# Routed rows placed in units of 128: 36 groups of two units in place of 39 groups of 256 rows

## The chip, the cores and the metric

The kernel runs on one core of a Trainium2 chip. A time is device microseconds (us) from start to end of one execution. Times are given as the median of several runs. The profile describes one further execution, with a time of its own. On the chip, TensorE (PE) does the matmuls, VectorE (DVE), ScalarE (ACT) and GpSimd (POOL) the elementwise work, and SyncE (SP) issues most of the DMA transfers. PEld is TensorE's loading of a matmul's stationary operand.

## The reference: what is computed

Two transformer layers on 8 x 512 tokens of width 256. Each layer adds attention and a mixture of experts to its input. In both layers every token goes to two of eight experts. Cut to what matters:

```python
def _L0_ffn_ref(x, Wg, Wu, Wd, W1, W2):            # F = 512
    topv, topi = top_k(softmax(xt @ Wg), 2)
    topv = topv / sum(topv)
    y = gelu(xt @ Wu[e]) @ Wd[e]                   # of the two experts chosen
    return gelu(xt @ W1) @ W2 + sum of y * weight

def _L1_ffn_ref(x, router_w, router_b, w1, b1, w2, b2):   # F = 1024
    top_w, sel = top_k(xf @ router_w + router_b, 2)
    gates = softmax(top_w)
    out_i = gelu(xf @ w1[i] + b1[i]) @ w2[i] + b2[i]
    return sum of out_i * gate_i over the two chosen

xn = layernorm(x);  x = x + L0_attn(xn) + L0_ffn(xn)
xn = layernorm(x);  x = x + L1_attn(xn) + L1_ffn(xn)
```

The 4096 tokens make 8192 routed rows in each layer. How many rows an expert gets is known only on the chip, so the number of groups that the program runs is the largest that could be needed.

## The kernel before, in words

**Routing.** `Routing.choose` finds each token's two experts on DVE. `Routing.places` (lines 291 to 367) counts the rows of each expert with two matmuls and a scan, rounds each expert's count up to groups of GT = 256 rows, and gives every routed row its place in a buffer in HBM (`xd`) in which each expert's rows begin at a multiple of 256. `NG_MAX` (line 36) is (8192 + 8 * 255) // 256 = 39 groups. `self.eid` holds each group's expert. `Routing.send` scatters the normalized rows to their places with 64 indirect DMAs of POOL per layer.

**One group** (`Experts`, lines 449 to 655). `load` reads the group's expert number into a register, loads that expert's weights as one tile of the tag `ew` (1024 KB in layer 0, 2180 KB with the biases in layer 1), and loads the group's 256 rows (`xg`; in layer 1 also `xe`, the rows' routing columns). `turn` transposes the rows (TensorE in layer 0, DVE in layer 1) and works out where the results go. `up` does the first matmul, one weight block of 128 x 128 against 256 columns of rows at a time, and the gelu on ACT (line 582 in layer 0, two blocks at once; line 578 in layer 1, one block, because of the bias). `down` does the second matmul for each half of 128 rows, scales by the gate, in layer 1 adds the bias `b2` out of the weight tile (line 616), and POOL scatters the result to HBM (line 625). A float32 matmul is two instructions ("passes") in the profile, so a group of layer 1 is 32 passes of `up` and 32 of `down`, and one of layer 0 16 and 16.

**Layer 0.** The groups are worked on between the steps of attention. A loop over n (lines 1033 to 1102) has one stage for each of 32 units of attention: four heads of one block of 512 tokens. In stage n the scores of unit n+1 are computed for their maxima (`maxima`, with DVE's reduction, line 836), and unit n's probabilities (`probs`, with ACT's exp, line 861), and between these stand other steps out of the deque `between`: norms, projections, the `down` of the groups of stage n-1, the `turn` of those of stage n. The `up` of stage n's groups comes at its end, and then the loads of the groups two further on. A stage begins with `shift(n)`, whose DVE subtraction is line 848. Groups of a shared expert fill the stages before 8 and after 27. `groups_of` (line 984) spreads the routed groups over stages 8 to 27: two for each stage, and one for stage 27. The routing of layer 0 is one step of stage 2.

**Layer 1.** Half of attention runs first (`attention1`, part "a", with the routing of layer 1 as one of its steps), then all groups in one stretch (`Experts.all`, lines 640 to 655), then the other half of attention. The program of that stretch is, for group i: the load of i+2, the turn of i+1, `up(i)`, `down(i-1)`. The weights' pool has three buffers (line 1387). A load that has no free buffer waits until the last reader of an earlier group's weights, line 616, is done. The order on each engine's queue is made when the program is built, from dependencies, priorities and expected times, so it can differ from the order in which the program writes its steps.

Of the kernel before, what the change touches and what calls it, by code (L numbers as in the profile page):

```python
# [17 lines left out]
P = 128  # L18
# [16 lines left out]
GT = 256  # L35
NG_MAX = (2 * B * S + E1 * (GT - 1)) // GT
TT = B * NT
# [10 lines left out]
C_THR = C_ONES + P  # L48
C_GRP = C_THR + B * S // GT
C_KEEP = C_GRP + NG_MAX  # L50
C_ROW = C_KEEP + TT
C_ALL = C_ROW + NG_MAX * GT // P

# [15 lines left out]
def tile_two_layers(  # L69
# [51 lines left out]
    ones = cs[:, C_ONES : C_ONES + P]  # L121
    thr = cs[:, C_THR : C_THR + B * S // GT]
    grp = cs[:, C_GRP : C_GRP + NG_MAX]
    keep = cs[:, C_KEEP : C_KEEP + TT]
    rowno = cs[:, C_ROW : C_ROW + NG_MAX * GT // P]

# [77 lines left out]
    class Routing:  # L204

        def __init__(self, layer):
            n = self.layer = layer
            self.asked, self.fetched = {}, set()  # L210
            self.sent, self.posted = [], []
            self.lg = rpool.tile([P, TT, 8], F32, tag="lg", name=f"lg{n}")
            self.hot = [
                rpool.tile([P, TT, 8], F32, tag=f"hot{k}", name=f"hot{n}_{k}") for k in range(2)
            ]

            self.of = rpool.tile([P, TT, 3, 2], F32, tag="of", name=f"of{n}")
            self.g = [rpool.tile([P, TT], F32, tag=f"g{k}", name=f"g{n}_{k}") for k in range(2)]
            self.pos = [rpool.tile([P, TT], I32, name=f"pos{n}_{k}") for k in range(2)]
            self.eid = rpool.tile([P, NG_MAX], I32, name=f"eid{n}")  # L220
            self.ef = rpool.tile([P, NG_MAX], F32, name=f"ef{n}")

            self.spare = rpool.tile([P, NG_MAX * GT // P], F32, tag="spare", name=f"spare{n}")
            self.xn_d = dpool.tile([B, P, NT, D], F32, name=f"xn_d{n}")
            self.xd = dpool.tile([NG_MAX * GT, XW], F32, name=f"xd{n}")
            self.zd = dpool.tile([1 + 2 * PLANE + NG_MAX * GT, D], F32, name=f"zd{n}")
# [64 lines left out]
        def places(self, ps_pool):  # L291


            def by_expert(ap):
# [14 lines left out]
            upto = self.small("upto", 8, TT)  # L309
            reset = self.small("reset", 8, TT)  # L310
            nc.vector.tensor_copy(reset, keep.unsqueeze(1).to_broadcast([P, 8, TT]))
# [7 lines left out]
            )  # L319
            m = B * S // GT  # L320
            over = self.small("over", 8, m)
            nc.vector.tensor_tensor(
                over,
                upto[:, :, TT - 1].unsqueeze(2).to_broadcast([P, 8, m]),
                thr.unsqueeze(1).to_broadcast([P, 8, m]),
                ALU.is_gt,
            )
            groups = self.small("groups", 8)
            nc.vector.tensor_reduce(groups, over, AX.X, ALU.add)
            end = self.small("end", 8)  # L330
            nc.vector.tensor_tensor_scan(end, ones[:, :8], groups, 0.0, ALU.mult, ALU.add)

            nc.vector.tensor_sub(groups, end, groups)
            nc.vector.scalar_tensor_tensor(
                upto,
                groups.unsqueeze(2).to_broadcast([P, 8, TT]),
                float(GT),
                upto,
                ALU.mult,
                ALU.add,  # L340
            )
            nc.vector.tensor_sub(upto, upto, tot)
            nc.vector.tensor_tensor(
# [3 lines left out]
                ALU.add,  # L347
            )
            for k in range(2):
                part = self.small("rest", TT, 8)  # L350
                nc.vector.tensor_tensor(
                    part, self.hot[k], upto.rearrange("p e t -> p t e"), ALU.mult
                )
                row = self.small("row", TT)
                nc.vector.tensor_reduce(row, part, AX.X, ALU.add)
                nc.vector.tensor_copy(self.pos[k], row)
            done = self.small("done", NG_MAX, 8)
            nc.vector.tensor_tensor(
                done,
                end.unsqueeze(1).to_broadcast([P, NG_MAX, 8]),  # L360
                grp.unsqueeze(2).to_broadcast([P, NG_MAX, 8]),
                ALU.is_le,
            )
            of = self.small("of", NG_MAX)
            nc.vector.tensor_reduce(of, done, AX.X, ALU.add)
            nc.vector.tensor_scalar_min(self.ef, of, 7.0)
# [82 lines left out]
    class Experts:  # L449


        def __init__(self, routing, e_d, wpool, pool, ps_x, ps_up, ps_dn, nf, bias, tag=None):
# [6 lines left out]
            self.post = lambda step: step()  # L459

        def load(self, i):
            r = self.r
            e = nc.sync.value_load(r.eid[0:1, i : i + 1], min_val=0, max_val=7)
            n_all = self.n_up + self.n_dn + (self.nf + D if self.bias else 0)
            w = self.wpool.tile([P, n_all], F32, tag="ew", name=f"ew{r.layer}_{i}")
            nc.sync.dma_start(w, self.e_d[bass.ds(e, 1)].rearrange("o p n -> p (o n)"))
            self.weights[i] = w
            if self.blocks:
# [57 lines left out]
        def address(self, i, of):  # L526
# [4 lines left out]
            mine = self.pool.tile([P, n_t, 2], F32, tag="mine", name=f"mine{n}_{i}")  # L531
            nc.vector.tensor_scalar(
                mine, of[:, :, 0], self.r.ef[:, i : i + 1], None, ALU.is_equal
            )
# [19 lines left out]
        def up(self, i, f2):  # L554
            n, w = self.r.layer, self.weights[i]
            wu = w[:, : self.n_up].rearrange("p (k f) -> p k f", k=KD)
            xt = self.xts[i]
            if f2 == 0:
                self.hts[i] = self.pool.tile(
                    [P, self.nf, GT], F32, tag="hgT", name=f"hgT{n}_{i}"  # L560
                )
            ht = self.hts[i]
            ps = self.ps_up.tile([P, 2, GT], F32, tag=self.tag[1], name=f"gup{n}_{i}_{f2}")
            for j in range(2):
                f = 2 * f2 + j
                for k in range(KD):
                    nc.tensor.matmul(  # L567
                        ps[:, j, :],
                        wu[:, k, f * P : (f + 1) * P],
                        xt[:, k],  # L570
                        start=(k == 0),
                        stop=(k == KD - 1),
                    )
            if self.bias:
                at = self.n_up + self.n_dn
                for j in range(2):
                    f = 2 * f2 + j
                    nc.scalar.activation(  # L578
                        ht[:, f, :], ps[:, j, :], AF.Gelu, bias=w[:, at + f : at + f + 1]
                    )  # L580
            else:
# [4 lines left out]
        def down(self, i, t, held={}):  # L586
            n, nf = self.r.layer, self.nf
            w = self.weights[i]
            wd = w[:, self.n_up : self.n_up + self.n_dn]
            wd = wd.rearrange("p (f d) -> p f d", f=nf)  # L590
            ht = self.hts[i]
# [13 lines left out]
            if t == GT // P - 1:  # L605
# [5 lines left out]
                for s in range(GT // P):  # L611
                    g = way[:, s, 1:2]
                    if self.bias:
                        nc.scalar.activation(y[:, s, :], ps[:, s, :], AF.Copy, scale=g)  # L614
                        b2 = w[:, self.n_up + self.n_dn + nf :]
                        nc.vector.scalar_tensor_tensor(  # L616
# [23 lines left out]
        def all(self):  # L640
            self.load(0)
            self.load(1)
            self.turn(0)
            for i in range(NG_MAX):
                if i + 2 < NG_MAX:
                    self.load(i + 2)
                if i + 1 < NG_MAX:
                    self.turn(i + 1)
                for f2 in range(self.nf // 2):
                    self.up(i, f2)  # L650
                if i:
                    for t in range(GT // P):
                        self.down(i - 1, t)
            for t in range(GT // P):
                self.down(NG_MAX - 1, t)

# [68 lines left out]
    with tc.tile_pool(name="l0w", bufs=1) as awp, tc.tile_pool(  # L725
# [254 lines left out]
        shared = deque(("shared", i) for i in range(B * S // GT))  # L980
        experts = deque(("routed", i) for i in range(NG_MAX))
        FIRST, LAST = 8, 27
# [43 lines left out]
        def loading():  # L1026
            move(len(moves))
            routed.load(0)
            routed.load(1)

        norms = deque(s for b in range(1, B) for s in norm_steps(b))
        downs = []
        for n in range(-1, N + 1):
# [57 lines left out]
            for group in groups:  # L1091
# [3 lines left out]
                kind, i = group  # L1095
                if kind == "routed" and i + 2 < NG_MAX:
                    routed.load(i + 2)
            if FIRST < n <= FIRST + CLEAR:
# [287 lines left out]
    attention1(list(range(B // 2)), "a", before, lambda b: None)  # L1386
    with tc.tile_pool(name="m1w", bufs=3) as wp, tc.tile_pool(
        name="m1", bufs=2
# [7 lines left out]
def _shape_constants():  # L1396
# [12 lines left out]
    c[:, C_ONES : C_ONES + P] = 1.0  # L1409
    c[:, C_THR : C_THR + B * S // GT] = GT * np.arange(B * S // GT)  # L1410
    c[:, C_GRP : C_GRP + NG_MAX] = np.arange(NG_MAX)
    c[:, C_KEEP : C_KEEP + TT] = np.arange(TT) > 0
    c[:, C_ROW :] = P * np.arange(NG_MAX * GT // P)[None, :] + p[:, None]

# [78 lines left out]
```

## Time and profile before

| | us |
|---|---|
| median of 3 runs | 2071.28 |
| the 3 runs | 2068.76, 2071.28, 2080.68 |
| the profiled execution, its own time | 2069.25 |
| its span, first to last instruction | 2067.6 |

| stretch of the profiled execution | us | PE busy | granted TensorE clock |
|---|---|---|---|
| 0 to 320: set-up, first stages of layer 0's attention, shared groups | 320 | 265.20 | 0.95 |
| 320 to 930: stages with the routed groups of layer 0 | 610 | 589.38 | 0.99 |
| 930 to 1060: last stages, adding the routed results, norms | 130 | 92.53 | 0.81 |
| 1060 to 1319: attention of layer 1, part a | 259 | 215.24 | 0.88 |
| 1319 to 1330: wait for the first rows and weights | 11 | 0.00 | 0.56 |
| 1330 to 1873: the groups of layer 1 | 543 | 542.80 | 1.00 |
| 1873 to 2067.6: attention of layer 1, part b | 194.6 | 169.08 | 0.97 |

A line of the profile gives the line of the program, the engine, the operation, the tile written and those read, the shapes and the count. Busy time adds the durations of instructions. TensorE's instructions overlap: a pass of 256 columns is shown with 0.38 us, but 32 in a row take 7.07 us. In a timeline, instructions of one kind that follow each other are merged into one line: start, length, engine, line, what, count.

### The profile page before, as it was taken

The numbers are of one execution on the slowest core, as the hardware profiler recorded it, in microseconds if no ns is written. First come the engines' busy times: TensorE is split into PE (matmuls) and PEld (weight loads), VectorE is DVE, ScalarE is ACT, GpSimd is POOL, SyncE is SP. The second block draws the span as 40 slices with busy tenths as digits, with TensorE's granted clock in tenths as the row PEclk, the third lists the DMA queues.
The fourth block names the chain that finished last, engine by engine and source line by source line (L and its number), as shares of the span: only waits on it lengthen the run. The fifth ranks groups of instructions, "written<-read, shape, count | busy, mean of one in ns | idle before, by whom it ended". The sixth has DMA issues, their size and how long they took to land. (4 is left out here: it accounts for less than half of the span.)

```text
span 2067.6 us, 27795 instructions
## 1 busy us (share of the span) xinstructions
PE 1874.2 (91%) x10452; PEld 1281.4 (62%) x10452; DVE 834.5 (40%) x1822; ACT 788.0 (38%) x1390; POOL 534.8 (26%) x581
## 2 busy tenths in 40 slices
PE   5887999999999999997776798799999999997998
PEld 3434656566666666654443455588888888884555
DVE  5453334343444434344666555311121111115765
ACT  2332443343434444443334344333322332232544
POOL 2024531221221222121234685011111111114332
PEclk9998999999999999998788889899999999999999
DMA  8932322674533344223212231446556655642400
GB/s 234 197 98 91 94 76 55 174 202 115 163 123 113 112 135 132 87 99 94 81 57 77 81 101 47 146 163 215 195 189 212 215 193 191 211 153 93 131 11 21
DMA packets 166806, 267.67 MB, mean 129 GB/s; under 512 B 67840, under 2 KB 140816, under 8 KB 156688
## 3 DMA queue, kind: packets, MB, share of 16 engines
q1 hardware_dynamic: 150976, 225.74, 36.1%
q0 software_dynamic: 13664, 37.64, 5.0%
q10 hardware_dynamic: 2032, 2.52, 0.4%
q8 instruction: 82, 1.34, 0.3%
q14 instruction: 52, 0.43, 0.1%
HBM read 182.12 MB, written 71.13 MB: 122 GB/s over the span
## 5 line engine op out<-in xcount | busy, mean ns | idle before, releaser
L567 PE MATMUL gup<-xgT,ew 128*128 128x256 f32 x1872 | 426.7, 383 | 14.1 <-DVE xgT L501 11.6
L598 PE MATMUL gdn<-ew,hgT 128*128 128x256 f32 x1872 | 428.5, 383 | 0.0
L567 PEld LDWEIGHTS gup<-xgT,ew 128*128 128x128 f32 x1872 | 352.7, 191 | 75.2 <-issue 20.0
L598 PEld LDWEIGHTS gdn<-ew,hgT 128*128 128x128 f32 x1872 | 353.3, 191 | 59.7 <-issue 13.5
L836 DVE TENSOR_REDUCE mx<-m 128x4 f32<-128x2048 f32 (+3 forms) x128 | 190.1, 1485 | 276.6 <-PE m L835 276.5
L625 POOL DMA_INDIRECT zd<-yo,row x156 | 151.5, 971 | 514.0 <-DVE yo L616 461.1
L863 POOL TENSOR_SCALAR_AFFINE_SELECT pt<-pt 128x512 f32<-128x512 f32 x128 | 81.7, 638 | 682.4 <-ACT pt L861 682.3
L861 ACT ACTIVATE pt<-s 128x2048 f32<-128x2048 f32 (+3 forms) x128 | 158.4, 1237 | 215.5 <-PE s L857 215.0
L578 ACT ACTIVATE hgT<-gup,ew 128x256 f32<-128x256 f32 x312 | 130.9, 471 | 160.0 <-PE gup L567 106.4
L831 PE MATMUL m<-k,q 32*128 32x512 f32 (+3 forms) x1024 | 126.7, 505 | 40.3 <-ACT pt L861 21.1
L857 PE MATMUL s<-qsh,k 32*128 32x512 f32 (+3 forms) x1024 | 112.6, 496 | 35.7 <-DVE mx L836 22.3
L382 POOL DMA_INDIRECT xd<-xr,pos x128 | 127.3, 995 | 36.0 <-issue 32.1
L616 DVE SCALAR_TENSOR_TENSOR yo<-ew,way,yo 128x256 f32<-128x256 f32 x78 | 34.6, 482 | 203.3 <-ACT yo L614 203.3
L861 ACT ACT_TABLE_LOAD x50 | 64.2, 1283 | 133.3 <-PE s L857 132.4
L614 ACT ACTIVATE yo<-gdn,way 128x256 f32<-128x256 f32 x78 | 32.7, 470 | 213.3 <-PE gdn L598 213.3
L831 PEld LDWEIGHTS m<-k,q 32*128 32x128 f32 x1024 | 50.9, 191 | 97.0 <-ACT pt L861 55.6
L501 DVE STREAM_TRANSPOSE xgT<-xg 128x512 f32<-128x512 f32 x39 | 27.6, 709 | 190.8 <-DMA xg<-xd 120.4
L857 PEld LDWEIGHTS s<-qsh,k 32*128 32x128 f32 x1024 | 42.6, 189 | 90.7 <-DVE mx L836 57.7
L890 DVE STREAM_TRANSPOSE ou<-av 128x512 f32<-128x512 f32 x32 | 22.9, 716 | 171.7 <-PE av L881 171.6
L881 PE MATMUL av<-pt,vaug 128*32 128x256 f32 (+3 forms) x1024 | 84.5, 443 | 3.1 <-POOL pt L863 3.0
L1244 ACT ACTIVATE u<-cs,lf 128x128 f32<-128x128 f32 x256 | 81.6, 394 | 3.3 <-DVE lf L1187 3.3
L1275 PE MATMUL a<-qb,qkTs 128*128 128x512 f32 x128 | 69.4, 625 | 10.8 <-DVE qb L1268 8.9
(194 smaller groups left out, 2416.2 us busy)
## 6 DMA issues: line engine op xcount, KB each, us to landing
ew<-in_dram SPq DMA_DIRECT2D x39, 2180.0 KB, 9.3
ew<-in_dram SPq DMA_DIRECT2D x39, 1024.0 KB, 4.9
xd<-zero SPq DMA_DIRECT2D x12, 1703.0 KB, 13.1
z<-zd SPq DMA_DIRECT2D x32, 512.0 KB, 5.0
xg<-xd SPq DMA_DIRECT2D x39, 262.0 KB, 3.4
xg<-xd SPq DMA_DIRECT2D x156, 64.0 KB, 8.5
xn_d<-l_xn SPq DMA_DIRECT2D x16, 512.0 KB, 4.1
xr<-xn_d SPq DMA_DIRECT2D x16, 512.0 KB, 4.6
```

The lines of the kernel that those rows point to most:

```text
L382: i = nc.gpsimd.indirect_dma_start(out=self.xd, out_offset=bass.IndirectOffsetOnAxis(ap=self.pos[k][:, at : at + 1], axis=0), in_=held[b][ ...
L567: nc.tensor.matmul(ps[:, j, :], wu[:, k, f * P : (f + 1) * P], xt[:, k], start=(k == 0), stop=(k == KD - 1),)
L578: nc.scalar.activation(ht[:, f, :], ps[:, j, :], AF.Gelu, bias=w[:, at + f : at + f + 1])
L598: nc.tensor.matmul(ps[:, t, :], ht[:, f, t * P : (t + 1) * P], wd[:, f, :], start=(f == 0), stop=(f == nf - 1),)
L625: d = nc.gpsimd.indirect_dma_start(out=self.r.zd, out_offset=bass.IndirectOffsetOnAxis(ap=row[:, s : s + 1], axis=0), in_=y[:, s, :], in_o ...
L831: nc.tensor.matmul(ps[:, h, :w], q[r, j * P : w], k[r, :w], start=True, stop=False)
L836: last["dve"] = nc.vector.tensor_reduce(mxs[n % 2][:, j, :, HD0], ps[:, :, :w], AX.X, ALU.max)
L857: nc.tensor.matmul(ps[:, h, :w], k[r, i * P : (i + 1) * P], q[r, i * P :], start=True, stop=True)
L861: nc.scalar.activation(e, ps[:, :, :w], AF.Exp, scale=0.25)
L863: last["pool"] = nc.gpsimd.affine_select(out=e[:, :, :P], in_=e[:, :, :P], pattern=[[0, 4], [1, P]], base=0, channel_multiplier=-1, compar ...
L881: nc.tensor.matmul(ps[32 * h : 32 * h + 32, i * P :], vaugs[b % 2][:, i, c : c + 32], e[:, h, :], start=(i == 0), stop=(i == NT - 1),)
L1244: nc.scalar.activation(u[:, h, :], inc, AF.Copy, scale=lf[:, c, h : h + 1])
```

## The change

An expert's rows are now counted in units of P = 128. A group is still 256 rows, two units. There are at most NU = 72 units, so 36 groups. The first `PURE` = 25 groups are whole groups of one expert, as many as there must be at least. Behind all whole groups come the units that are left, at most two of each expert, side by side. The last 11 groups, the mixed ones, hold any further whole groups and these units, and may have one expert in the first half and another in the second. Each mixed group therefore loads two sets of weights, also where both halves have the same expert. They are worked on at the positions `MIXED` of the order, between the others.

In a mixed group `up` runs each weight block against 128 columns, once for each half with that half's weights; in layer 1 the gelu is split by halves too, because the bias differs. `down` was by halves before and takes the weights of its half. In layer 0 the second set of weights goes into `xnT` of blocks 0 to 3, no longer in use by then. In layer 1 both sets are buffers of the weights' pool, which has four in place of three. `places` counts whole groups and left-over units apart, and every row of a left-over unit is moved behind the whole groups. With 36 groups, `groups_of` gives one group in place of two to stages 12, 17 and 22.

The diff, cut to its core:

```diff
-NG_MAX = (2 * B * S + E1 * (GT - 1)) // GT
+NU = -(-((2 * B * S + E1 * (P - 1)) // P) // 2) * 2
+NG_MAX = NU // 2
+PURE = -(-(2 * B * S - E1 * (GT - 1)) // GT)
+MIXED = (3, 8, 12, 15, 18, 21, 24, 27, 29, 32, 35)
+def order_of_groups():
+    pure, mixed = list(range(PURE)), list(range(PURE, NG_MAX))
+    return [mixed.pop(0) if j in MIXED else pure.pop(0) for j in range(NG_MAX)]
+ORDER = order_of_groups()
...
         def places(self, ps_pool):
-            m = B * S // GT
-            over = self.small("over", 8, m)
+            m = B * S // P
+            n_of = upto[:, :, TT - 1]
+            over = self.small("at", 8, m)
+            whole = self.small("groups", 8)
+            n_gt = m * P // GT
+            nc.vector.tensor_tensor(
+                over[:, :, :n_gt],
+                n_of.unsqueeze(2).to_broadcast([P, 8, n_gt]),
+                thr[:, 2 :: 2].unsqueeze(1).to_broadcast([P, 8, n_gt]),
+                ALU.is_ge,
+            )
+            nc.vector.tensor_reduce(whole, over[:, :, :n_gt], AX.X, ALU.add)
...
+            rest = self.small("left", 8)
+            nc.vector.tensor_reduce(rest, over, AX.X, ALU.add)
+            nc.vector.tensor_scalar_mul(whole, whole, 2.0)
+            nc.vector.tensor_sub(rest, rest, whole)
...
+            nc.vector.tensor_tensor(
+                late, upto, whole.unsqueeze(2).to_broadcast([P, 8, TT]), ALU.is_ge
+            )
...
+            h = NU // 2
+            for i in range(2):
+                for lo in (0, h):
+                    us = slice(lo, lo + h)
+                    done = self.small("done", h, 8)
...
+                    nc.vector.tensor_reduce((ends if i else of)[:, us], done, AX.X, ALU.add)
...
         def load(self, i):
-            self.weights[i] = w
+            w = self.weights_of(2 * i)
+            if i < PURE:
+                self.weights[i] = w, w
+            else:
+                self.weights[i] = w, self.weights_of(2 * i + 1, self.second and self.second(i))
...
         def up(self, i, f2):
+            parts = [(0, GT)] if i < PURE else [(0, P), (P, P)]
...
+                for u, (at, m) in enumerate(parts):
+                    for k in range(KD):
+                        x = xt[:, k]
+                        x = x[:, at // 32 : (at + m) // 32] if self.blocks else x[:, at : at + m]
+                        nc.tensor.matmul(
+                            ps[:, j, at : at + m],
+                            wu[u][:, k, f * P : (f + 1) * P],
+                            x,
+                            start=(k == 0),
+                            stop=(k == KD - 1),
+                        )
             if self.bias:
...
+                    for u, (at, m) in enumerate(parts):
+                        nc.scalar.activation(
+                            ht[:, f, at : at + m],
+                            ps[:, j, at : at + m],
+                            AF.Gelu,
+                            bias=w[u][2][:, f : f + 1],
+                        )
...
         def down(self, i, t, held={}):
-            wd = w[:, self.n_up : self.n_up + self.n_dn]
-            wd = wd.rearrange("p (f d) -> p f d", f=nf)
+            wd = w[t][1].rearrange("p (f d) -> p f d", f=nf)
...
         def all(self):
+            o = ORDER
+            for j, i in enumerate(o):
+                if j + 2 < NG_MAX:
+                    self.load(o[j + 2])
+                if j + 1 < NG_MAX:
+                    self.turn(o[j + 1])
...
-        experts = deque(("routed", i) for i in range(NG_MAX))
+        experts = deque(("routed", i) for i in ORDER)
+        mixed = sorted(range(PURE, NG_MAX), key=ORDER.index)
+        places = [xnT[0:2], xnT[0:2]] + [xnT[2:4], xnT[0:2]] * len(mixed)
+        routed.second = lambda i: places[mixed.index(i)]
...
-    with tc.tile_pool(name="m1w", bufs=3) as wp, tc.tile_pool(
+    with tc.tile_pool(name="m1w", bufs=4) as wp, tc.tile_pool(
```

## The prediction, made blind

> **What bounds the kernel now.** I read the sums by stretch first, then the costliest groups of instructions, then TensorE's timeline in the stretches that the change touches. Sums by stretch, of layer 1's groups alone (us, busy time of PE, PEld, DVE, ACT, POOL, granted clock, DMA share, GB/s):
>
> ```profile
> 1330.20:1857.30 527.10, 527.10 (x2432) 463.16 (x2433) 88.98 (x307) 162.39 (x385) 71.92 (x74) 1.00 0.59 197
> ```
>
> TensorE never stops there, every other engine is idle most of the time, and DMA is at 0.59. The timeline of TensorE in the middle of it (start, length):
>
> ```profile
> 1463.83 7.07 PE L567 MATMUL gup<-xgT,ew 128*128 128x256 f32 x32
> 1470.74 7.07 PE L598 MATMUL gdn<-ew,hgT 128*128 128x256 f32 x32
> 1477.65 7.07 PE L567 MATMUL gup<-xgT,ew 128*128 128x256 f32 x32
> ```
>
> From one `up` to the next is 1477.65 - 1463.83 = 13.82 us for 64 passes, 0.216 us a pass (the 0.383 us of the group list overlaps). 39 groups make 539 of the 543 us: a group taken away here is 13.8 us, as long as weights come in time.
>
> Do they? From the waits of SP's queue (total, times, longest) and from the page's list of transfers (count, size, us to landing):
>
> ```profile
> SPq L466 <- DVE yo L616: 288.3, 36, 15.2
> ```
> ```profile
> ew<-in_dram SPq DMA_DIRECT2D x39, 2180.0 KB, 9.3
> ```
>
> Each load waits for the last reader of an older buffer. The one after the block ending at 1463.83 is issued at 1465.54, 1.7 us later, and lands 9.3 us after that: 11.0 of the 13.8 us that it has. So 2.8 us are spare.
>
> At the start of the stretch TensorE does this:
>
> ```profile
> 1330.20 9.01 PE L567 MATMUL gup<-xgT,ew 128*128 128x256 f32 x32 [11.56 <-DVE xgT L501]
> 1339.05 4.91 PE L598 MATMUL gdn<-ew,hgT 128*128 128x256 f32 x22
> 1343.80 7.07 PE L567 MATMUL gup<-xgT,ew 128*128 128x256 f32 x32
> ```
>
> Only group 0's `up` is done when the second line runs, so 22 of its 32 `down` passes stand before `up(1)`, against the program's order. The queue as built puts `down` forward when it expects weights late. This matters below.
>
> Layer 0, by stages, each from one subtraction of line 848 to the next (stages 23, 24, 27, 28):
>
> ```profile
> 779.40:805.80 26.40, 25.58 (x180) 16.71 (x180) 11.29 (x24) 14.59 (x15) 6.31 (x8) 1.00 0.41 134
> 805.80:840.00 34.20, 33.90 (x224) 22.15 (x228) 15.58 (x29) 10.05 (x12) 6.50 (x9) 1.00 0.34 106
> 900.40:924.40 24.00, 21.80 (x161) 13.60 (x162) 10.49 (x19) 10.67 (x11) 5.48 (x7) 1.00 0.22 73
> 924.40:952.10 27.70, 27.50 (x174) 15.33 (x173) 13.00 (x18) 11.67 (x12) 5.18 (x7) 1.00 0.30 89
> ```
>
> TensorE is busy nearly throughout, but includes short waits for DVE's maxima and ACT's exp. Stages with less work for it show what a group is worth.
>
> **Part by part. Three groups fewer in layer 1.** 3 x 13.82 = -41.4 us.
>
> **The halved `up` of mixed groups.** In place of 32 passes of 256 columns (16 in layer 0) come 64 (32) of 128, each with a weight load of its own: (64 + 32) x 11 = 1056 short passes. The cost hangs on whether the load hides behind a pass as short as itself. The nearest rows (PEld is the load):
>
> ```profile
> 1306.33 0.30 PEld L1316 LDWEIGHTS pm<-v,kw 128*128 128x128 f32 x2 [0.20 <-issue]
> 1306.34 0.49 PE L1316 MATMUL pm<-v,kw 128*128 128x128 f32 x2
> 1306.55 0.36 PEld L1248 LDWEIGHTS qkT<-cs,qk 128*128 128x128 f32 x3
> 1306.66 0.49 PE L1248 MATMUL qkT<-cs,qk 128*128 128x128 f32 x3
> ```
>
> From the first load (1306.33) to the next matmul's start (1306.66) pass 0.33 us for two passes: one exposed load and two passes of 0.11, the second load hidden. The three qkT passes take 0.49; one alone shows 0.27 (0.273 median of the like row at L517), so they follow at (0.49 - 0.27) / 2 = 0.11. Two short passes thus cost 0.216, one long one. A rule of the Trainium skill speaks against this: "TensorE: Matmul & The Clock Gate", section Back-to-back issue gap, says that in a stream of load and matmul pairs a 128-column matmul takes about 81 ns where the array alone needs 56, since the load counts too. Scaled to these rows (an estimate: 0.108 x 25 / 56 = 0.048 us more each) that is 1056 x 0.048 = +51 us. Fully serial loads would give 1056 x 0.108 = +114. The rows are of this kernel and of this shape, only in short runs: I take 0, range 0 to +114, most weight at 0.
>
> **ACT.** Layer 1's mixed groups have 16 gelus of 128 columns for 8 of 256. The nearest row, L1244's 128 x 128, has 0.394 us: 6.3 us a group for 3.8 (8 x 0.471). It runs beside an `up` of 6.9 us, so nothing is added; without that cover it would be 11 x 2.5 = 28. In layer 0 the gelus stay as they were.
>
> **Second weights in layer 1.** 11 loads more. DMA moved 405 GB/s while a load filled it (1606.5 to 1611), so 2180 KB (2.23 MB) behind another take 5.5 us. As a share: 0.59 x 527 us, less three groups, plus 11 x 5.5, over some 490 us is about 0.7; DMA does not become the bound. Timing may. With three consecutive groups, one of them mixed, all four buffers are taken until the oldest group's `down` ends, so both loads of mixed positions 15, 18, 21, 24, 27, 32 and 35 start together: 1.7 + 9.3 + 5.5 = 16.5, 2.7 us late, seven times 19. Positions 3, 8 and 12 find one buffer free earlier: no delay. Position 29 follows 27 by two, which asks for five buffers; its second set starts when its `up` is due, 11 us late, and after that pause TensorE restarts slowly as at 1330.20 (9.01 for 7.07): 13. Together +32 in the program's order. SP's later loads queue behind such a wait, and DVE's transpose L501 behind the rows, but these too serve later groups. If the queue is built with `down` ahead, as at 1339.05, 6.9 us of work cover each 2.7, and buffers come free half a group earlier. Doubling a load must make the builder expect it late, since at the start it does so with single ones. Left are 11 - 6.9 = 4 us at position 29 and 1 elsewhere: +5 taken, range 0 to +32.
>
> **Layer 0.** A group is 32 passes (6.9) and four transposes (4 x 0.108): 7.35 us. Stage 27 has one `up` and two transposed blocks less than stage 23, 3.9 us of TensorE, and is 2.4 shorter (62%). Stage 28 lacks 7.8 us of stage 24's passes and is 6.5 shorter (83%). At 73%, stages 12, 13, 17, 18, 22 and 23 give 3 x 7.35 x 0.73 = -16 (bounds: a third, -7, and all, -22). The 11 extra loads of 1 MB (2.6 us each at 405 GB/s) come one stage ahead, but the q and k pieces for the next unit (line 820) queue behind them on SP; this trace shows TensorE waiting on these for 16 us in this stretch, so +2 (0 to +5): -14.
>
> **`places`.** By its rows (0.42 us for 256 elements, 0.48 for 312, 0.16 for 8) the added DVE steps are 8.8 us and the removed ones 2.2: +6.6 twice. They run between reductions that TensorE waits for (L836; layer 1: L1268, L1276). I take 4 of each 6.6: +8, range +2 to +13. The sends that wait for the places end at 1287, well before 1319.
>
> Costed at nothing: register loads and issues on SP (0.4 us each, inside its waits), the zeroing in 12 rows for 13, 12 scatters fewer (POOL 74 of 543 us busy), line 532's comparison.
>
> **Sum.** 2069.25 (the profiled execution, span 2067.6) - 41.4 + 0 + 5 - 14 + 8 = 2027. The median shown is 2 us above that execution: 2029.
>
> **Rivals.** (a) The order stays: +32 in place of +5, 2056. For it: that is the order at 1463 to 1484. Against it: 1339. (b) Loads of weights don't hide behind short passes: 2029 + 114 = 2143 fully serial, slower. The place is L567 in mixed groups; it decides from 42 / 1056 = 0.04 us extra a pass, an interval of 0.15. The scaled rule, at 0.048, lands at 2080. Against it: the rows above. (c) Layer 0's stages are bound by the chain of maxima and exp, so their groups return nothing: 2043. For it: stage 27's 62%; against it: stage 28. (d) The groups left out were not work on the path: 2071 or more; excluded in layer 1, where TensorE is busy 527 of 527 us.
>
> **Chances.** Mine 0.57, (a) 0.23, (b) 0.09, (c) 0.11. 0.5% is 10 us, about what a measurement of this kernel can tell from no change. Mine and (c) are faster; (a), 15 us under the median with 10 us of its own spread, is faster in half its cases and the same in most others; (b) is slower but for its smallest sizes. Faster 0.79, same 0.12, slower 0.09. Range: no stalls, all of layer 0 and +2 for `places` give about 2010; the top of (a) is 2064.
>
> **What would show it.** `up` of a mixed group at 64 passes in about 7.0 us: right; 9 or more: (b). Gaps before L567 of 2 to 4 us at every third group and about 11 at the 30th: (a); L598 before L567 there with no gap: mine. Stages 12, 17, 22 no shorter than 16, 21, 18: (c). I am wrong altogether if the queue order or the buffers' waits come out otherwise than either case.

## The result, and the profile after

| | us |
|---|---|
| before, median of 4 runs beside the changed kernel | 2072.05 (2068.76 to 2080.68) |
| changed, median of 4 runs | 2041.68 (2040.34 to 2043.17) |
| ratio, 95% interval | 0.9853 (0.9823 to 0.9882) |
| the profiled execution of the changed kernel, its own time | 2040.34 (span 2038.6) |

The prediction was 2029, range 2010 to 2064. The total lies inside, 13 us above; its parts do not lie where the prediction put them. The spans of the two profiled executions differ by 2067.6 - 2038.6 = 29.0 us:

| stretch (stages count from the subtraction of `shift`) | before | after | difference | prediction |
|---|---|---|---|---|
| start to stage 8 (first routed groups) | 311.2 | 301.8 | -9.4 | +4 (`places`) |
| stages 8 to 27, the groups of layer 0 | 613.2 | 590.9 | -22.3 | -14 |
| stages 28 to 30 | 108.6 | 113.8 | +5.2 | 0 |
| from there to the first `up` of layer 1 | 297.2 | 300.0 | +2.8 | +4 (`places`) |
| the groups of layer 1 | 541.3 | 535.3 | -6.0 | -36.4 (-41.4 + 0 + 5) |
| attention of layer 1, part b | 196.1 | 196.8 | +0.7 | 0 |

The groups of layer 1 are counted here from their first matmul to the end of their last, in every kernel. Before, that end is at 1871.5; the 1873 used further up is 1.5 us into part b.

So layer 1's groups gave a sixth of what was forecast, and the part ahead of them gave far more. Layer 1's groups in the changed kernel, as sums of the stretch (us, busy time of PE, PEld, DVE, ACT, POOL, granted clock, DMA share, GB/s):

```profile
1306.50:1841.80 535.30, 510.48 (x2657) 454.71 (x2658) 78.68 (x284) 164.30 (x447) 67.90 (x70) 0.99 0.63 225
```

TensorE, which never stopped here before, is busy 510.48 of 535.30 us. TensorE's waits of that stretch (total, times, longest) say for what:

```profile
PE gup L649 <- DVE mine L605: 34.7, 12, 11.5
PE gup L649 <- DMA ew<-in_dram: 1.7, 1, 1.7
```

One of the twelve is the start (11.5). The other 11 are 2.1 us each, and DVE is named, not the weights. Ten of them stand ahead of the `up` of a mixed group, one ahead of the whole group behind position 29. The mixed group at position 29 has the one wait for weights, 1.7 us, in the middle of its `up`. TensorE's timeline around one of the eleven, at position 12 (start, length; what ended the idle time):

```profile
1462.90 7.07 PE L649 MATMUL gup<-xgT,ew 128*128 128x256 f32 x32
1469.80 10.09 PE L682 MATMUL gdn<-ew,hgT 128*128 128x256 f32 x46
1482.00 7.41 PE L649 MATMUL gup<-xgT,ew 128*128 128x128 f32 x64 [2.10 <-DVE mine L605]
```

A mixed group's `up` (64 short passes) stands behind 46 passes of `down`: the queue does put `down` forward, as the prediction expected, and still TensorE pauses. All engines in the last microseconds ahead of the first such pause, at position 3:

```profile
1347.82 2.54 PE L682 MATMUL gdn<-ew,hgT 128*128 128x256 f32 x11
...
1350.39 0.84 ACT L698 ACTIVATE yo<-gdn,way 128x256 f32<-128x256 f32 x2 [6.07 <-PE gdn L682]
1350.90 0.88 DVE L700 SCALAR_TENSOR_TENSOR yo<-ew,way,yo 128x256 f32<-128x256 f32 x2 [6.03 <-ACT yo L698]
...
1351.70 0.70 DVE L574 STREAM_TRANSPOSE xgT<-xg 128x512 f32<-128x512 f32 x1
...
1352.46 0.71 PE L649 MATMUL gup<-xgT,ew 128*128 128x128 f32 x4 [2.10 <-DVE mine L605]
```

`down` ends, ACT scales its result, DVE adds the bias to it (L700), and only then does DVE transpose the mixed group's rows (L574), which the next `up` reads. Those rows were there 10 us earlier: their packets end at 1341.2, those of both sets of weights at 1340.0. DVE was idle for 6 us ahead of L700. The transpose stood behind L700 in DVE's queue, and so TensorE waited for its own last result to pass ACT and DVE. The profile names L605, the step behind the transpose.

The first blocks of the stretch answer to those shown of before; the pause at the start, 11.53 for 11.56, is unchanged:

```profile
1306.50 9.32 PE L649 MATMUL gup<-xgT,ew 128*128 128x256 f32 x32 [11.53 <-DVE mine L605]
1315.66 4.91 PE L682 MATMUL gdn<-ew,hgT 128*128 128x256 f32 x22
```

The waits of SP's queue in that stretch, and the page's row of the weights' transfers: 47 loads (36 and 11), landing in 9.7 us for 9.3, so the second sets did not crowd the transfers.

```profile
SPq L530 <- DVE yo L700: 250.1, 32, 18.2
```
```profile
ew<-in_dram SPq DMA_DIRECT2D x47, 2180.0 KB, 9.7
```

Stages 23, 24, 27 and 28 of layer 0, as shown of before (26.40, 34.20, 24.00, 27.70 there). Of these only stage 23 has less to do (one `down` less, from stage 22, which lost a group: 23.53 us busy for 25.58), and it takes as long; stages 12, 13, 17, 18, 22 and 23 together lost 18.2 us, for the 16 forecast:

```profile
746.10:772.50 26.40, 23.53 (x181) 15.23 (x175) 11.14 (x23) 13.90 (x14) 3.96 (x6) 0.98 0.25 81
772.50:808.40 35.90, 34.85 (x240) 22.51 (x243) 14.65 (x29) 10.15 (x12) 6.92 (x9) 0.96 0.40 133
869.10:892.70 23.60, 22.04 (x177) 14.46 (x174) 10.35 (x19) 11.96 (x12) 5.47 (x7) 1.00 0.35 117
892.70:921.10 28.40, 27.27 (x173) 15.19 (x172) 13.20 (x17) 12.85 (x13) 4.77 (x7) 1.00 0.31 90
```

### The profile page after: what moved, and what is told of

It reads as the page before. It is cut to its first block, busy times and chain, and to the rows that moved or that the text cites. A ratio compares the mean times of both kernels' runs of the same rounds, so it can differ in the third digit from the quotient of the medians.

```text
span 2038.6 us, 28372 instructions
## 1 busy us (share of the span) xinstructions
PE 1830.6 (90%) x10680; PEld 1248.1 (61%) x10680; DVE 826.3 (41%) x1821; ACT 785.7 (39%) x1441; POOL 522.9 (26%) x569
## 4 chain that ended last, share of the span: by engine, by line
PE 38%; DVE 7%; POOL 5%; issue 3%; DMA 2%; ACT 2%; SPq 0%; DVEq 0%; ACTq 0%; POOLq 0%
PE gup L649 12%; PE gdn L682 11%; POOL xd L437 2%; PE a L1365 2%; PE pa L1235 1%; DMA xg<-xd 1%; PE d L1351 1%; PE po L1428 1%; PE pb L1235 1%; PE y L1390 1%; DVE x L476 1%; DVE qb L1358 1%; PE m L916 1%; PE sup L1026 1%; POOL qk L1259 1%
## 5 line engine op out<-in xcount | busy, mean ns | idle before, releaser
L649 PE MATMUL gup<-xgT,ew 128*128 128x256 f32 (+1 forms) x2080 | 391.1, 342 | 38.6 <-DVE mine L605 34.8
L649 PEld LDWEIGHTS gup<-xgT,ew 128*128 128x128 f32 x2080 | 333.6, 194 | 86.3 <-DVE mine L605 27.5
L682 PE MATMUL gdn<-ew,hgT 128*128 128x256 f32 x1640 | 375.3, 383 | 0.0
L682 PEld LDWEIGHTS gdn<-ew,hgT 128*128 128x128 f32 x1640 | 308.8, 191 | 51.6 <-issue 11.7
L709 POOL DMA_INDIRECT zd<-yo,row x144 | 139.7, 970 | 512.6 <-DVE yo L700 483.5
L660 ACT ACTIVATE hgT<-gup,ew 128x256 f32<-128x256 f32 (+1 forms) x376 | 134.2, 423 | 266.2 <-issue 175.7
L700 DVE SCALAR_TENSOR_TENSOR yo<-ew,way,yo 128x256 f32<-128x256 f32 x72 | 31.7, 482 | 425.0 <-ACT yo L698 425.0
L946 ACT ACT_TABLE_LOAD x51 | 65.4, 1283 | 119.9 <-PE s L942 119.0
L1259 POOL TENSOR_TENSOR qk<-ra,rb 128x512 f32<-128x512 f32 x32 | 43.9, 1371 | 133.0 <-DVE rb L1256 109.3
L1235 PE MATMUL pa<-wcat,xnT 128*128 128x512 f32 x128 | 65.8, 628 | 8.1 <-DVE z L1263 6.2
```

The source lines that it names most:

```text
L649: nc.tensor.matmul(ps[:, j, at : at + m], wu[u][:, k, f * P : (f + 1) * P], x, start=(k == 0), stop=(k == KD - 1),)
L660: nc.scalar.activation(ht[:, f, at : at + m], ps[:, j, at : at + m], AF.Gelu, bias=w[u][2][:, f : f + 1],)
L682: nc.tensor.matmul(ps[:, t, :], ht[:, f, t * P : (t + 1) * P], wd[:, f, :], start=(f == 0), stop=(f == nf - 1),)
L709: d = nc.gpsimd.indirect_dma_start(out=self.r.zd, out_offset=bass.IndirectOffsetOnAxis(ap=row[:, s : s + 1], axis=0), in_=y[:, s, :], in_o ...
L946: nc.scalar.activation(e, ps[:, :, :w], AF.Exp, scale=0.25)
L1235: nc.tensor.matmul(ps[:, : c1 - c0], xnT[b][:, k, t * P : (t + 1) * P], wcat[:, k, c0:c1], start=(k == 0), stop=(k == KD - 1),)
```

## The experiments

### Is it DVE's queue or the late weights? The transpose first

In layer 1 the bias step of `down` may not stand ahead of the transpose of the group after it (the expectation below says "second group after it"; counted from the group of that result it is the next one).

```diff
+            self.turns.append(last["turn"])          # in turn_blocks
...
-                        nc.vector.scalar_tensor_tensor(
+                        with tc.issue_after(self.turns[-2].ins):
+                            nc.vector.scalar_tensor_tensor(
```

> The changed kernel with one edit in the order of DVE's queue: in layer 1 the addition of the bias for a group's result may not be queued ahead of the transpose of the second group after it. Its TensorE order and its transfers stay those of the changed kernel. Theory A: the pauses of 2.1 us before each mixed group's first matmul come from DVE's queue, where the mixed group's transpose stands behind the results of the group before. Then they vanish: 12 x 2.26 = -27 us, and up to -5 more, since the three mixed blocks at a halved clock after such a pause have no pause to follow: 2010 to 2017. Theory B: the pauses are the late second weights. Then they stay, and the time is 2041 as for the changed kernel, within 3.

2010.58 us (2010.09 to 2011.54), ratio 0.9711 (0.9689 to 0.9733). Layer 1's groups take 508.3 us for 535.3: -27.0. The same block as above; over the whole stretch TensorE's passes stand in the same order as in the changed kernel:

```profile
1462.68 10.09 PE L684 MATMUL gdn<-ew,hgT 128*128 128x256 f32 x46
1472.61 7.31 PE L651 MATMUL gup<-xgT,ew 128*128 128x128 f32 x64
1479.76 6.64 PE L684 MATMUL gdn<-ew,hgT 128*128 128x256 f32 x30
```

No pause. Ten of the eleven are gone; the one left (2.1 us) is ahead of the last group, which the edit doesn't reach, since no later transpose moves the list on. A wait of 1.6 us for weights stays at position 29. Theory A is shown: the edit moves a step of DVE and no transfer.

### The same by the order of the loads

```diff
         def load(self, i):
+            if self.blocks:
+                self.load_blocks(i)
             w = self.weights_of(2 * i)
...
             if self.blocks:
-                self.load_blocks(i)
                 return
```

> The changed kernel, but in layer 1 each group's rows are loaded ahead of its weights, not behind them. Theory A (DVE's queue order, made when the program is built from expected times, is the cause): the rows are expected earlier, the transposes move ahead of the results of the group before, and the pauses before the mixed groups go: 2010 to 2020. Theory B (the second weights come late): they come later still by the rows' transfer, pauses stay or grow: 2041 to 2050.

2006.73 us (2004.05 to 2009.91), ratio 0.9697 (0.9672 to 0.9723); repeated beside other runs (below) 0.9696. With the rows issued ahead of the weights, the builder sets the transpose ahead by itself, as it would if it expects the rows earlier. It laid out TensorE anew as well: a mixed `up` now begins behind 30 passes of `down` and is split (16 passes, some of `down`, then 48), so this run alone would not single out DVE's queue. Layer 1's groups take 504.3 us. One pause is left, in the middle of the mixed group at position 29, and this one is the weights':

```profile
1705.66 1.95 PE L650 MATMUL gup<-xgT,ew 128*128 128x128 f32 x16
1707.45 1.03 PE L683 MATMUL gdn<-ew,hgT 128*128 128x256 f32 x4
1710.52 5.62 PE L650 MATMUL gup<-xgT,ew 128*128 128x128 f32 x48 [2.04 <-DMA ew<-in_dram]
```

So second weights cost 2 us, at the one place where the prediction found too few buffers.

### The halved `up`

The kernel before, each `up` of both layers in halves with the same weights:

```diff
-                for k in range(KD):
-                    nc.tensor.matmul(ps[:, j, :], ...
+                for at in (0, P):
+                    for k in range(KD):
+                        nc.tensor.matmul(ps[:, j, at : at + P], ...
```

> The kernel before, with the first matmul of every one of its 39 groups of both layers in two halves of 128 rows with the same weights, the gelu unsplit: 39 x 96 = 3744 short passes for 1872 long ones. The prediction's rate (nothing extra): 2071. The changed kernel's mixed groups take 7.25 us from start to the next block for 6.91, which is 0.005 us extra a short pass: +13 in layer 1 (39 x 0.34) and up to +7 in layer 0, 2085 to 2091. The skill's rule, scaled as in the prediction (0.048 us extra a short pass): +180, 2250.

2085.9 us (2085.61 to 2088.58), ratio 1.0079 (1.0055 to 1.0103). In the trace, one block and the next:

```profile
1598.84 7.31 PE L570 MATMUL gup<-xgT,ew 128*128 128x128 f32 x64
1605.98 7.07 PE L601 MATMUL gdn<-ew,hgT 128*128 128x256 f32 x32
```

1605.98 - 1598.84 = 7.14 for the 6.91 of whole blocks: 0.23 a group, 0.0036 us a short pass. Layer 1's groups take 550.3 for 541.3 us (+9.0, which is 39 x 0.23), stages 8 to 27 take 615.6 for 613.2 (+2.4). The other 5 us of the span's difference lie in stages 28 to 30 and part b, which the edit doesn't touch. For the change's 11 groups this is 11/39 of 11.4: 3 us. In this kernel a load of weights hides nearly whole behind a pass as short as itself.

### 36 groups and nothing else

```diff
+NG_RUN = 36
-            for i in range(NG_MAX):
+            for i in range(NG_RUN):                  # likewise in layer 0
```

The last three groups' rows are left out.

> The kernel before, but only the first 36 of its 39 groups are worked on in each layer; the rows of the last three are left out, as are the mixed groups and all other parts of the change. It gives the price of a group alone. The prediction's terms: -41.4 in layer 1 and -16 in layer 0, 2014. If layer 0's stages were bound by the chain of maxima and exp (rival c): -41, 2030. If stages without a group give all of their 7.35 us: 2008.

2013.93 us (2010.50 to 2016.67), ratio 0.9729 (0.9703 to 0.9755). Layer 1's groups take 500.8 us for 541.3, -40.5; stages 8 to 27 take 598.8 for 613.2, -14.4. Both terms hold in size, and rival (c) (-41 alone) is out: stages 13, 17, 18 and 22 are 3.0 to 3.5 us shorter each. But not all of the 14.4 is work left out: the six stages that have an `up` or a `down` less (12, 13, 17, 18, 22, 23) give 12.6, stage 19 takes 3.0 more, and 5.3 come from stage 14, which has all its groups and lost its wait for pieces of k (2.8 us in the trace of before).

### The extra gain in layer 0: SP's queue, twice

Groups left out give 14.4 us in stages 8 to 27, yet the change gave 22.3, and 9.4 ahead of them. Two places stood out. In stage 10 TensorE waited 3.6 us for pieces of k, which stood on SP behind the rows of later groups and the zeroing; in the changed kernel they stand ahead. SP ahead of stage 10, in the kernel before (it begins at 372.9) and in the changed one (363.6):

```profile
362.11 0.90 SPq L472 DMA_DIRECT2D xg<-xd  x2
363.05 0.46 SPq L183 DMA_DIRECT2D xd<-zero  x1
364.98 5.40 SPq L820 DMA_DIRECT2D k<-raw  x4
```
```profile
355.51 2.43 SPq L905 DMA_DIRECT2D k<-raw  x4
358.03 1.07 SPq L545 DMA_DIRECT2D xg<-xd  x2
```

Why the builder set them ahead there stays open.

In stage 3 the expert numbers are read into SP's registers, one read after another, ahead of the next pieces of k. SP's reads in that stretch of before and of the changed kernel (duration min/median/max in ns, first and last start):

```profile
L463 SPq TENSOR_LOAD <-eid x32: 262/268/727, 141.0 to 161.1; - x32
```
```profile
L520 SPq TENSOR_LOAD <-eid x24: 262/272/605, 139.3 to 154.7; - x24
```

31 of the 32 stand behind the last weight load, from 142.2, at 0.62 us from one to the next. Before, the pieces of k go out at 161.98, although TensorE's last step on the old k had ended at 154.4; in the changed kernel, with 22, at 155.52.

The first place, in the kernel before: rows and zeroing behind the pieces.

```diff
+            with behind("spread"):
                 last["load"] = nc.sync.dma_start(x, ...
...
+                with behind("spread"):
                     clear(1, n - FIRST - 1)
...
-                    nc.sync.dma_start(held[n % 2]...
+                    last["spread"] = nc.sync.dma_start(held[n % 2]...
```

> The kernel before with one edit in SP's queue: the loads of the groups' rows and the zeroing of layer 1's buffer may not be queued ahead of the pieces of q and k that the program issues before them. In the kernel before the pieces of k for stages 10, 12 and 14 stand behind them, and TensorE waits up to 3.6 us for these; in the changed kernel they stand ahead. Theory: this order, and not the groups left out, is the part of layer 0's gain above the 14.4 us that 36 groups alone gave: stage 10 takes 30 us for 35.9, stages 12 and 14 31 for 35.0 and 36.2, in all 10 to 15 us, 2055 to 2060 against 2070. Rival: the order costs nothing, since matmuls move around it: 2068 to 2072.

2066.27 us, ratio 0.9956 (0.9942 to 0.9969), about -9 us. Stages 10 and 14 take 30.0 us each, for 36.9 and 36.3 in the kernel before beside it; stage 12 stays (36.1 for 36.3), which I had wrong. Stages 8 to 27: 603.7 for 615.0, -11.3. TensorE's longest waits of 300 to 925, in the kernel before on that chip and with the edit:

```profile
PE m L831 <- DMA k<-raw: 9.0, 3, 3.6
PE s L857 <- DVE mx L836: 7.7, 16, 0.6
```
```profile
PE s L858 <- DVE mx L837: 9.7, 18, 0.6
PE m L832 <- ACT pt L862: 2.5, 2, 1.7
```

The wait for k is gone, and stage 10 takes 30.0 us as in the changed kernel. The -14.4 of 36 groups and these -11.3 must not be added, since both hold stage 14. What the changed kernel has beyond 36 groups is 7.9 us: 6.6 in stage 10, which this run shows to be the order on SP; 4.1 in stage 12 (31.1 for 35.2), which neither run shortens by itself; and some 3 lost in the others.

The second place, in the kernel before: a register read may not stand ahead of the loads of the group before.

```diff
-            e = nc.sync.value_load(r.eid[0:1, i : i + 1], min_val=0, max_val=7)
+            with behind("load"):
+                e = nc.sync.value_load(r.eid[0:1, i : i + 1], min_val=0, max_val=7)
```

> The kernel before with one edit in SP's queue: the register load of a group's expert number may not be queued ahead of the loads of the group before. In the kernel before, 31 of the 39 register loads of layer 0 stand in a row on SP as soon as the numbers are there (141.8 to 162.0, 0.65 us each), ahead of the pieces of k that the next maxima wait for; in the changed kernel 22 do. Theory A: these cost the kernel before its stall of 5.5 us in stage 3, and are why the changed kernel's stage 3 is 10.8 us shorter. Then stage 3 takes 28 to 33 us for 39.0 here, and the time is 2060 to 2065. Theory B: stage 3 is shorter in the changed kernel because its routing's DVE steps fell into another place. Then stage 3 stays at 38 to 39 and the time at 2070.

2077.67 us, ratio 1.0007 (0.9993 to 1.0021): no change, though stage 3 took 28.6 us. Stages 4 to 7 took 9 us longer than in the trace of before. So they did in all four kernels that ran on this chip (126 to 129 us for 118), and in none of the other ten traces (117 to 119). So the kernel was run again on another chip, beside a trace of the unchanged one.

> The kernel before, unchanged, so that its trace stands on the same chip as the runs beside it: between the runs so far, stages 4 to 7 of layer 0 took 118 us in one group of runs and 126 to 129 in the other, whatever the kernel. If that is the chip and not the kernels, these stages take here what they take in the other runs of this call. Time 2068 to 2080.

2073.68 us, one run; stages 4 to 7: 117.4. Stage 3: 36.3, with a wait of 4.6 us ahead of the maxima. The profile names no releaser for it, but it ends 2 us after k goes out (SP and TensorE):

```profile
166.08 2.42 SPq L820 DMA_DIRECT2D k<-raw  x4
168.05 3.98 PE L831 MATMUL m<-k,q 32*128 32x512 f32 x8 [4.61 <-issue]
```

> The same kernel as the one with the register loads held back, which came out at no change (1.0007) although its stage 3 took 28.6 us for the 39.0 of the kernel before: its stages 4 to 7 took 9 us longer. If the longer stages are the chip's, the ratio here is again 1.000 only if the kernel before has them too and another loss makes up for stage 3; if they belong to the edit, stages 4 to 7 are again 9 us longer than in the kernel before beside it. A real gain of stage 3 alone would be 10 us, a ratio of 0.995.

2071.65 us (20 runs), ratio 0.9979 (0.9971 to 0.9987), about -4 us. The same two steps:

```profile
154.85 2.40 SPq L821 DMA_DIRECT2D k<-raw  x4
158.75 1.24 PE L832 MATMUL m<-k,q 32*128 32x512 f32 x8
```

Stage 3 takes 27.3 us (-9.0), stages 4 to 7 117.5. So the longer stages were not the edit's; that they belong to the chip of those four kernels would fit, but no trace of the kernel before was taken there, and it stays open. Stages 8 to 27 take 619.1 for 615.0 us: with the reads next to the weight loads, TensorE's wait for k there grows from 9.0 to 12.8 us. The reads ahead of k are shown to cost stage 3 its 9 us; merely put elsewhere, they cost some of it there. How the number of reads ahead of k bears on stage 3 is put together under the next run.

### The price of `places`

Steps that change no value, as many as the change adds, in the routing of before:

```diff
+            for _ in range(8):
+                nc.vector.tensor_max(end, end, end)
...
+            for _ in range(6):
+                nc.vector.tensor_max(upto, upto, upto)
...
+            for _ in range(4):
                 done = self.small("done", NG_MAX, 8)     # and its comparison and sum
```

> The kernel before with DVE steps added to the routing of both layers that change no value: 6 steps of 256 elements, 8 of 8, and the 312-element comparison with its sum three times more, about 6.6 us by the rows of before, as many as the change adds. The prediction's term: 4 us on the path in each layer, +8 (2 to 13): 2079. If the routing's steps gave back in stage 3 what they cost in stage 2, as the two stages together suggest (59.5 us for 61.2, theory B of the run beside this one): 2068 to 2073. By theory A the register loads only start later here, so nothing comes back: 2078 to 2083.

2089.33 us (2087.85 to 2093.83), ratio 1.0065 (1.0045 to 1.0086): +13. Stage 2 takes 34.3 us, for 28.4 with the reads held back on the same chip; the stretch from stage 31 to layer 1's first `up`, which holds the routing of layer 1, takes 306.1 for 295.4. (The expectation above gives 59.5 for 61.2 us for stages 2 and 3 together; counted as here they are 61.1 in the changed kernel and 65.4 in the kernel before.) Stage 3 takes 29.4 us, so it does give something back, and my theory A ("the register loads only start later") is wrong on this point: in the queue as built only 18 reads, not 31, are left ahead of the pieces of k, since the numbers are expected later. Over the runs, with the reads ahead of k in the queue as built:

| reads ahead of k | kernels | stage 3, us |
|---|---|---|
| 31 | before (two traces), the halves, 36 groups, rows behind the pieces | 36.3 to 39.0 |
| 22 | changed, transpose first, rows first (two traces), three buffers | 28.2 to 32.9 |
| 18 | more steps in `places` | 29.4 |
| none in a row | reads held back (two traces), and in the best version | 27.3 to 28.8 |

So the change's shorter stage 3 fits its longer routing, which sets later in SP's queue what stood ahead of k. In the changed kernel and its variants stage 2 took 30.3 to 32.9 us (six traces, mean 31.5), in the kernel before and its variants without added steps 26.4 to 28.4 (seven, mean 27.1): +4.4. The stretch from stage 31 to layer 1's first `up` took 296.6 to 303.7 (mean 300.4) for 293.1 to 298.3 (mean 296.3): +4.1. That is the size of the term, 4 and 4. But in the same traces all that lies ahead of stage 2 is 4.7 us shorter in the changed kernels (123.7 for 128.4), so that stage 2 ends at the same time, 155.2 for 155.5. Whether the steps cost layer 0 anything, or work only moved across the stage's boundary, is not separated. The steps added in this run cost more than the change's; that they stand in one chain may be why, which is not shown.

### Holding the reads back in the best version

> The changed kernel with two edits: in layer 1 the rows are loaded ahead of the weights, and a register load may not be queued ahead of the loads of the group before. Theory A: stages 2 and 3 lose what the 22 register loads still cost, 1 to 5 us of the 2006.7 us that the first edit alone has: 2001 to 2006. Theory B: 2007. A loss is possible if the register loads, now next to each weight load, hold up other transfers on SP: up to 2015.

2016.72 us, ratio 0.9718 (0.9699 to 0.9736), against 0.9697 and 0.9696 without: no gain is seen. Stage 3 is shorter (28.8 for 32.6 and 29.8). But this run was on the chip with the long stages 4 to 7 (127.7), and the other two were not.

### Three buffers of weights in place of four

> The changed kernel with the rows loaded ahead of the weights in layer 1, and three buffers of weights there in place of four. A mixed group's second set can then start only when the group two before has done its last matmul, some 11 us of matmuls ahead of its use, and takes 11 to 16.5 us. The prediction's arithmetic for late weights: 0 to 5 us for each of 11 mixed groups, 2007 to 2062, 2035 the middle. If second weights need no fourth buffer: 2007.

2088.77 us, one run (before, beside it: 2076.41): all that the change gave is lost. Layer 1's groups take 570.2 us for 504.3. This is what late weights look like. TensorE's waits there, the start's 11.4 among them:

```profile
PE gup L650 <- DMA ew<-in_dram: 48.5, 13, 11.4
PE gup L650 <- issue: 7.7, 3, 3.0
```

The pauses alone make about 45 us (525.4 of 570.2 us are busy). The rest: the same 2657 passes are busy 525.4 us for 502.3 with four buffers, 23 us more, at a granted clock of 0.96 over the stretch for 1.00. That was not in my arithmetic, which stopped at 2062.

### The best version again

> The best version so far again, the changed kernel with the rows loaded ahead of the weights in layer 1, on the chip of the runs beside it: ratio 0.967 to 0.973 to the kernel before, 2003 to 2013.

2013.22 us, ratio 0.9696 (0.9673 to 0.9719). The change with the rows loaded first is 3% faster than the kernel before, where the change as made is 1.5%.

## Why the prediction came out as it did

**Three groups fewer in layer 1, -41.4.** Right: -40.5 by themselves.

**The halved `up`, 0.** Right in kind: 64 passes in 7.14 to 7.25 us, for 7.0 forecast and 9 for rival (b). The exposed part is 0.0036 us a pass, 3 to 4 us in all, not 0. The rule of the Trainium skill that spoke against it ("TensorE: Matmul & The Clock Gate", section Back-to-back issue gap), scaled by the prediction to 0.048, was 13 times too dear here; the short rows of the trace decided rightly.

**ACT, 0.** Right; a gelu of 128 columns took 0.369 us, for 0.394 estimated, and TensorE never waits for it.

**Second weights in layer 1, +5.** The term that failed, in its mechanism: layer 1 lost some 32 us here. The weights themselves were right: `down` stands ahead, the DMA share is 0.63 to 0.68 for "about 0.7", and the one stall is at position 29, 2 us for 4. What the prediction passed over is its own clause that DVE's transpose stays "behind the rows, but these too serve later groups". When the builder moved `down` ahead of a mixed `up`, it set that `down`'s bias step on DVE ahead of the transpose as well, and so tied `up` to the end of `down`: 11 x (2.10 + 0.16) = 25 us, by TensorE's block ends. With the 1.7 for position 29 and three blocks at a lower clock (8.86 and twice 9.04 for 7.1 to 7.3, 5 us) that is 32. On the face of it the pauses have the place and the size that the prediction's last part gave to rival (a), late weights: 2 us at mixed groups. Taken by that alone, (a) would have been called confirmed. But (a) had no delay at positions 3, 8 and 12, where there are pauses of 2.1 us, and 11 us at the 30th group, where there are 1.7; and the releaser named in the waits, the packets' ends and the first two runs say otherwise. The sum for layer 1: -40.5 + 3.8 + 32 = -5, found -6.0.

**Layer 0, -14.** Near in size for the groups (-14.4), though 5.3 of that is stage 14's wait for k. Of the other 8 us, stage 10 is shown to be the order on SP, where the pieces of k now stand ahead of rows and zeroing; stage 12 is not explained. The prediction looked at this queue, saw waits for such pieces, and counted only a loss (+2). Its 16 us of waits are too many: it adds the waits of weight loads (8.4) to those of the matmuls behind them (7.2), which stood still for the same pieces.

**`places`, +8.** Stage 2 is 4.4 us longer and the stretch ahead of layer 1's groups 4.1, as forecast; for layer 0 that it is a loss on the path is not shown, since stage 2 ends no later. But stage 3 came out 10.8 us shorter, out of "register loads and issues on SP (0.4 us each, inside its waits)", costed at nothing: 0.62 us each, and 31 of them in one row ahead of TensorE's next operands. What shortened the time ahead of stage 2 by 5 us stays open.

So the total was nearly met by luck, because errors made up for each other: +30 in layer 1's groups (-6.0 for -36.4), -18 in all ahead of them (-23.7 for -6), +1 in part b, 13 in all. Stages 28 to 30, at +5.2, are no effect: the unchanged kernel's two traces have 108.6 and 112.6 there.

## What to carry to other kernels

When a change makes the builder expect one operand late, other queues can be laid out anew around that expectation, not only the one under study: list, for the engine that must not stop, each small step of another engine ahead of it, and what stands ahead of that step on its queue. Issue what is small and wanted soon (the rows, 0.26 MB) ahead of what is large (weights, 2 MB). Here that one move was worth as much as the whole change, but not because the rows had come late, since those of the first pause lay there 10 us early: the move changed the order that the builder gave DVE and TensorE. The ordering edit on DVE alone gave most of the same gain (508.3 us for 504.3). And a pause at the predicted place is no proof of the predicted cause: read its releaser and the landing of the operand it was blamed on.

## What was not expected of the hardware

A pause of 2.1 us was followed, in three of eleven cases, by some 3.4 us at a granted clock of 0.52, 0.53 and 0.66; in the other eight it was 1.00. The length of a pause did not decide it alone: with three buffers one of 3.0 us, at 1444.85, was followed by 30 short passes in 3.4 us, at 1.00. What did decide it stays open. Behind the pauses at 1570.10 and 1482.00 (granted clock third from the end):

```profile
1482.00:1485.50 3.50, 3.50 (x31) 3.50 (x32) 1.40 (x6) 1.14 (x4) 1.14 (x2) 1.00 1.13 320
1570.10:1573.50 3.40, 3.40 (x17) 3.40 (x18) 1.58 (x8) 0.00 (x0) 1.14 (x2) 0.53 1.16 344
```

17 short passes in the one, 31 in the other. With three buffers, where pauses were 2 to 4 us, TensorE's passes took 23 us longer. And a register read on SP costs that queue 0.62 us from one to the next, though its row shows 0.27.
